# Attention loads turned in place, memory loaded into its final tile, and the attention and routing of a quad gathered ahead of product 1

## The chip, the cores and the metric

The kernel runs on 1 core of a Trainium2 chip. The metric is the device time of one execution in microseconds (us); lower is better. PE is TensorE, PEld its weight loads, DVE is VectorE, ACT is ScalarE, POOL is GpSimd, and SP is the engine whose queue issues every DMA of this kernel.

## The reference, cut to what matters

All data is float32; x is 8 x 1024 x 1024, and each of the 8 batches has its own memory of 64 rows and a mask over them.

```python
scores = einsum('bsd,bmd->bsm', layernorm(x), memory) * scale   # masked, softmax over m
x = x + einsum('bsm,bmd->bsd', softmax(scores), memory)
h = layernorm(x)
base   = einsum('btd,od->bto', h, weight)
probs  = softmax(h @ router_w.T)            # 8 experts, the best 2, renormalised
Ax     = einsum('nd,erd->ner', h, lora_A)   # rank 16 for each expert
out    = x + base + 2 * einsum('ner,ne,eor->no', Ax, w_dense, lora_B)
```

## The kernel before, in words

**Tiles, pairs, quads.** The 8192 rows are 64 tiles of 128 rows. Two tiles are a *pair* (32 of them, four to a batch). After a start (`first`, pairs 0 and 1), the function `quad(u)` (L1128) works on the two pairs u and v = u+1 in one pass; it runs 15 times, for u = 2, 4, ..., 30. The dense product h x weight is done by Strassen's scheme in two levels: per quad seven *joint* products (`joint`, L817), run in the order 1, 2, 6, 3, 7, 5, 4, each of seven blocks of matmuls in two PSUM banks (named jl and ju). The sums that the products need are made by POOL (`rt_sums` L632, `rt_sum_3` L643, `joint_sums_steps` L793), and DVE, ACT and POOL take the results away. Product 1 leaves its result in the tile of its own operand (hA): the first part is copied there by ACT (L839), two others by DVE (L841), and matmuls of the same product reuse the bank only after such a copy.

**What one quad does.** Three generations of pairs are in flight. u and v: the two low-rank and router products (`rt_low_rank_tile`, L576), the choice of the experts (`rt_top`, L588: 15 small DVE operations and one ACT Exp in the middle), the turn of the scaled low-rank rows (`rt_turn_low_rank`, L617), a low-rank add of one quarter of the output (`eight`, L751), and the seven products. n = u+2 and m = u+3: the end of the attention (softmax of m, `att_turn_p`, readout = probabilities x memory, `att_add` into x), then layernorm 2 and the write and blocked re-read through DRAM (`f_rows`, `norm_send`, `norm_fetch`) that lets DVE turn h (`rt_turn_tile`). f = u+4 and g = u+5: the load of x in blocked form (`load_xs`, L96), its turn by DVE (`att_turn_tile`, L393), and the scores (`att_scores`, L400).

**What sets the order.** `tc.manual_schedule` (L1332): each engine, and SP's DMA queue, executes its instructions strictly in the order in which the program writes them. Tiles come from pools with a fixed number of buffers; an instruction that needs a buffer waits until its last reader is done. `ring` (5 buffers of 128 x 1024) holds the blocked loads xs, the turned x (xT), h on its way out, the re-read hs, and the blocked memory ms. `ps_at` and `ps_rt` are one PSUM buffer each: `ps_at` holds in turn the scores of f (sct), their turned form (sc) and turned probabilities; `ps_rt` holds the low-rank result (pa) and m's turned probabilities. Hooks are functions that `joint` calls between its blocks: with them the softmax of m (L1196, L1197) and the last turn of g (L1201) are put between blocks of product 1.

**Order in a late quad before** (u = 4 to 26; u = 2 is "early", u = 28 and 30 are the tail). PE: the last product's end of the quad before (`pending`), low-rank of u, the turn of m's scores (sc), low-rank of v, product 1, `rt_turn_low_rank(u)`, `eight(u)`, readout of n, turned probabilities of m, scores of f and g, readout of m, `rt_turn_low_rank(v)`, `eight(v)`, product 2, and so on. DVE: `rt_top(u)`, turns of f0 and f1, the shift of m's scores (L434, L439), turn of g0, product 1's copies mixed with the division of m's softmax and the turn of g1, then the adds. SP: at product 4 the first half of the output rows of u and v (two stores), `fetch_sums("w11")` (L696), the two x tiles of g, the blocked tiles f0, f1 and g0; then the second half of the output rows (two stores, `last`, L1323), then g1 and the two x tiles of f.

**Memory.** For a new batch `load_ms` (L343) loads the memory in blocked form into a ring slot, with runs of 1 KB, `turn_mem` (L353) turns it into memT, and `centre_turned` (L361) takes off the row means.

Of the kernel before, what the change touches and what calls it, by code (L numbers as in the profile page):

```python
# [17 lines left out]
P = 128  # L18
# [6 lines left out]
def kernel(  # L25
# [35 lines left out]

    const = ctx.enter_context(tc.tile_pool(name="const", bufs=1))
    xpool = ctx.enter_context(tc.tile_pool(name="xpool", bufs=10))
    ring = ctx.enter_context(tc.tile_pool(name="ring", bufs=5))
    turned = ctx.enter_context(tc.tile_pool(name="turned", bufs=2))
    sums = ctx.enter_context(tc.tile_pool(name="sums", bufs=1))
    memp = ctx.enter_context(tc.tile_pool(name="memp", bufs=2))
# [11 lines left out]
    def load_blocked(dst, rows):  # L79

        v = rows.rearrange("(t i) d -> i t d", i=NB)
        for q in range(4):
            nc.sync.dma_start(  # L83
                out=dst[q * NB : (q + 1) * NB], in_=v[:, :, q * QD : (q + 1) * QD]
            )
# [219 lines left out]

    mcs, mem_ts = {}, {}

    def mem_stats(b: int):
        mv = small.tile([P, 2], F32, tag="mv_mem", name=f"mv_mem_{b}", bufs=2)
        row_stats(mv[:M], mems[b][:M], f"mem_{b}", M)  # L310
        mcs[b, "mv"] = mv

    def centre_mem(b: int, chunks: bool):

        m = mems[b]
        if (b, "mv") not in mcs:
            mem_stats(b)  # L320
        mc = ring.tile([P, D], F32, tag="ring", name=f"memc_{b}_{chunks}")
# [13 lines left out]
    def turn_mem_pe(b: int, chunks: bool, mc):  # L335
# [4 lines left out]
        mem_ts[b, chunks] = mt  # L340
        return lambda: nc.scalar.copy(mt, tr)

    def load_ms(b: int):  # L343

        msr = ring.tile([P, D], F32, tag="ring", name=f"ms_{b}")
        n = M // NB * QD
        ms = msr[:, :n].rearrange("p (t c) -> p t c", c=QD)
        load_blocked(ms, mem[b])
        ones = msr[:, n : n + P]
        nc.gpsimd.memset(ones, 1.0 / D)  # L350
        mcs[b] = ms, ones, msr[:, n + P : n + P + M]

    def turn_mem(b: int):  # L353

        mt = memp.tile([P, KD, M], F32, tag="memT", name=f"memT_{b}_True", bufs=1)
        ms, ones, of_k = mcs[b]
        transpose_blocked(mt, ms)
        nc.vector.tensor_reduce(of_k, mt.rearrange("p k m -> p m k"), AX.X, ALU.add)
        mem_ts[b, True] = mt

    def centre_turned(b: int):  # L361

        _, ones, of_k = mcs.pop(b)
# [19 lines left out]

    def xT_tile(u: int, r: int):
        t = ring.tile([P, KD, P], F32, tag="ring", name=f"xT_{u}_{r}")
        x_ts.setdefault(u, []).append(t)
        return t

    def att_turn_pe(u: int, r: int, later: bool = False):
# [1 line left out]
        return transpose_pe((t[:, :KH, :], t[:, KH:, :]), xts[u][r], f"x{u}_{r}", later)  # L391

    def att_turn_tile(u: int, r: int):  # L393
        transpose_blocked(xT_tile(u, r), xss[u][r])

    def att_turn(u: int):
        for r in range(2):
            att_turn_tile(u, r)

    def att_scores(u: int, apart: bool = False):  # L400

        mt = mem_ts[u // PPB, u > 1]
        if apart:
            sct = bank_of(f"sct_{u}")[:, :P]
        else:
            sct = ps_at.tile([2 * M, P], F32, tag="at", name=f"sct_{u}")
        for k in range(KD):  # L410
            for r in range(2):
                mm(  # L412
                    sct[r * M : (r + 1) * M, :], mt[:, k, :], x_ts[u][r][:, k, :],
                    start=(k == 0), stop=(k == KD - 1),
                )
# [37 lines left out]
    def att_divide(u: int):  # L453
        s, of_s = ps[u]
        den, rden = of_s[:, 1], of_s[:, 2]
        nc.vector.reciprocal(rden, den)
        tt(s, s, rden.unsqueeze(2).to_broadcast([P, 2, M]), ALU.mult)
        ps[u] = s

    def att_turn_p(u: int, in_place: bool = False):  # L460
        if in_place:
            ptp = ps_rt.tile([2 * M, P], F32, tag="rt", name=f"ptp_{u}")
        else:
            ptp = ps_at.tile([2 * M, P], F32, tag="at", name=f"ptp_{u}")
# [81 lines left out]
    def hb_tile(u: int, r: int):  # L546
        if r == 0:
            h_tiles(u)
        t = turned.tile([P, KH, P], F32, tag="hB", name=f"hB_{u}_{r}", bufs=5)
        hbs[u].append(t)  # L550
        return t

# [17 lines left out]
            rt_low_rank_tile(u, r)  # L570

    def rt_low_rank_copy(u: int):
        axls[u] = small.tile([P, 2, ER + E], F32, tag="axl", name=f"axl_{u}", bufs=1)
# [84 lines left out]


    quarters, kept = {}, {}  # L660
    shared = const.tile([P, 3, HK, HH], F32, name="shared")

    def quarter(w, i: int, j: int):
        return w[:, i * HK : (i + 1) * HK, j * HH : (j + 1) * HH]
# [463 lines left out]
    def quad(u: int):  # L1128
# [25 lines left out]
            rt_low_rank_tile(u, 0)  # L1154
        rt_low_rank_tile(u, 1)
        if early:
            att_divide(n)
            att_turn_p(n)
            for r in range(2):
                rt_turn_tile(v, r)  # L1160
            rt_sums(v)
        rt_top(u)
# [6 lines left out]
        if early:  # L1169
            att_turn(m)  # L1170
        js_one, js_two = joint_sums_steps(1, u)
        js_one()
        rt_sum_3(u)
        rt_low_rank_tile(v, 0)
        if late and far:
            att_turn_tile(f, 0)
            load_xs(g, (1,))
            att_turn_tile(f, 1)
        if early:
            load_xs(f)  # L1180
        elif far:
            load_xt(f)
        rt_low_rank_tile(v, 1, later=True)
        rt_sum_3(v)
        js_two()
        if late:
            att_rstd(m)
            att_shift(m)
            if far:
                att_turn_tile(g, 0)  # L1190
        if early:
            att_scores(m)

        hooks = {2: [], 5: []}
        if late:
            hooks[2].append(lambda: att_exp(m))  # L1196
            hooks[5].append(lambda: att_divide(m))  # L1197
        if early:
            hooks[2].append(lambda: att_sc(m))
        elif far:  # L1200
            hooks[5].append(lambda: att_turn_tile(g, 1))  # L1201
        end_1 = joint(1, u, hooks, aside=not more)
        end_1()
        joint_sums(2, u)
        t_add(0, 0, u, v)
        still_one()
        rt_turn_low_rank(u, bank_of(f"trw_{u}")[:, : 2 * P])
        rt_low_rank_copy(v)
        eight(u)
        if early:  # L1210
            load_xs(g, (0,))
            att_rstd(m)
            att_exp(m)
            att_divide(m)
            att_turn_tile(f, 0)
            load_xs(g, (1,))
            load_xt(f)
            att_turn_tile(f, 1)
            att_turn(g)
        if more:  # L1220
            att_readout(n)
            att_turn_p(m, True)
        eight_add(u)
        if more:
            att_add(n)
        rt_top(v)
        if far:
            att_scores(f)
            att_scores(g, True)
        if next_mem:  # L1230
            load_ms((f + 2) // PPB)
        if more:
            att_readout(m)
            f_sums(n)
        if new_mem:
            load_mem(b)
        if more:
            att_add(m)
        rt_turn_low_rank(v, bank_of(f"trw_{v}")[:, : 2 * P])
        eight(v)  # L1240
        eight_add(v)

        hooks = {2: [], 5: []}
        if more:
# [135 lines left out]
```

## Time and profile before

| what | us |
| --- | --- |
| median of 3 runs (lowest to highest) | 1235.64 (1234.27 to 1235.87) |
| the profiled execution's own time | 1235.62 |
| span of that execution | 1233.8 |
| PE busy in the span | 1133.7 |
| DVE busy | 831.1 |
| POOL busy | 654.2 |
| ACT busy | 557.3 |
| mean granted TensorE clock | 0.968 |

The profiled execution agrees with the median, so what is read in it can be set against the runs. A quad takes some 75 us: the first low-rank matmul of the quad u = 16 starts at 640.15 us of the span, that of u = 18 at 714.87. Times within a quad are given below from that first low-rank matmul. Shares over the span average stages that differ, so a change in one stage is read from the timeline of that stage: what each engine does there, and which wait ends last.

### The profile page before, as it was taken

How to read it: one execution, taken by the hardware profiler on the slowest of the kernel's cores; microseconds unless marked ns; L12 is line 12 of the kernel's file. 1: busy time of each engine (PE TensorE's matmuls, PEld its weight loads, DVE VectorE, ACT ScalarE, POOL GpSimd, SP SyncE). 2: the span in 40 equal slices, each digit the busy share in tenths (PEclk: the TensorE clock that was granted, in tenths of full speed). 3: DMA queues.
4: the chain of work that ended last, by engine and by line, in shares of the span. 5: the costliest groups of instructions: out<-in, count | busy, mean ns of one | idle time of the engine just before them, and what ended most of it. 6: DMA issues, size and time to landing. Idle time of an engine off the chain costs nothing.

```text
span 1233.8 us, 17966 instructions
## 1 busy us (share of the span) xinstructions
PE 1133.7 (92%) x6044; PEld 892.2 (72%) x6044; DVE 831.1 (67%) x1979; ACT 557.3 (45%) x1063; POOL 654.2 (53%) x723
## 2 busy tenths in 40 slices
PE   8997898998989899898998989989898998989988
PEld 6555686885867768686786868868687786876867
DVE  7765668577684866858677585866858567565745
ACT  4584443725437353563625437253473625535000
POOL 0188385463654736556463664636547264564645
PEclk9999998998999989999999999999899998999989
DMA  9777347372565716547364482726637264432401
GB/s 235 176 214 226 99 145 222 126 237 82 178 189 162 230 69 213 159 158 237 93 208 137 149 252 100 226 85 205 197 123 242 81 207 151 137 136 85 164 26 69
DMA packets 109387, 198.42 MB, mean 161 GB/s; under 512 B 13424, under 2 KB 77936, under 8 KB 109296
## 3 DMA queue, kind: packets, MB, share of 16 engines
q1 hardware_dynamic: 109296, 197.28, 51.6%
q8 instruction: 48, 0.79, 0.3%
q14 instruction: 43, 0.35, 0.1%
HBM read 130.65 MB, written 66.58 MB: 160 GB/s over the span
## 4 chain that ended last, share of the span: by engine, by line
PE 70%; DMA 11%; DVE 8%; ACT 5%; issue 3%; SPq 2%; POOL 2%; DVEq 0%; ACTq 0%; POOLq 0%
PE jl L717 26%; PE ju L717 20%; DMA xs<-in_x_dram 6%; PE sct L412 5%; PE eight L709 3%; PE ju L709 3%; PE ro L480 3%; PE jl L709 3%; ACT junk L243 3%; PE pa L582 2%; PE plain L717 2%; DMA out_dram<-xt 2%; SPq L83 2%; DMA xt<-in_x_dram 2%; DVE xt L847 2%
## 5 line engine op out<-in xcount | busy, mean ns | idle before, releaser
L766 POOL TENSOR_TENSOR xt<-xt,hA 128x512 f32<-128x512 f32 x120 | 149.8, 1274 | 150.5 <-DVE hA L843 90.9
L847 DVE TENSOR_TENSOR xt<-jl,xt 128x256 f32<-128x256 f32 (+1 forms) x301 | 139.7, 484 | 131.4 <-PE jl L717 109.2
L717 PE MATMUL ju<-w,s_j 128*128 128x256 f32 x480 | 132.0, 399 | 32.0 <-DVE hA L841 31.8
L804 POOL TENSOR_TENSOR s_j<-s 128x256 f32<-128x256 f32 x45 | 32.8, 728 | 234.4 <-PE jl L717 204.3
L195 ACT ACTIVATE junk<-xt 128x1024 uint8<-128x1024 f32 x60 | 63.0, 1049 | 152.9 <-DMA xt<-in_x_dram 152.2
L717 PEld LDWEIGHTS ju<-w,s_j 128*128 128x128 f32 x480 | 89.8, 196 | 54.0 <-DVE hA L841 36.6
L847 DVE TENSOR_TENSOR xt<-ju,xt 128x256 f32<-128x256 f32 (+1 forms) x150 | 79.6, 547 | 43.2 <-PE ju L717 36.2
L843 DVE TENSOR_TENSOR hA<-jl,hA 128x256 f32<-128x256 f32 (+1 forms) x135 | 68.8, 510 | 55.6 <-PE jl L717 55.2
L638 POOL TENSOR_TENSOR s<-hA,hB 128x512 f32<-128x512 f32 x31 | 39.5, 1274 | 122.2 <-DVE hB L89 65.5
L296 ACT ACTIVATE h<-xt,of_f 128x1024 f32<-128x1024 f32 x60 | 71.3, 1235 | 58.9 <-DVE of_f L292 45.0
L706 DVE TENSOR_TENSOR xt<-ro,xt 128x512 f32<-128x512 f32 x128 | 82.1, 684 | 18.7 <-PE ro L480 18.7
L717 PE MATMUL ju<-t,s_j 128*128 128x256 f32 x360 | 93.8, 383 | 0.0
L582 PE MATMUL pa<-art_sb,hA 128*128 128x136 f32 x512 | 72.3, 285 | 8.2 <-ACT axl L574 7.9
L582 PEld LDWEIGHTS pa<-art_sb,hA 128*128 128x128 f32 x512 | 65.8, 192 | 13.3 <-ACT axl L574 11.2
L717 PEld LDWEIGHTS ju<-t,s_j 128*128 128x128 f32 x360 | 64.1, 190 | 15.4 <-issue 5.2
L89 DVE STREAM_TRANSPOSE xT<-xs 128x1024 f32<-128x1024 f32 x60 | 73.9, 1235 | 0.6
L582 PE MATMUL pa<-art_sb,hB 128*128 128x136 f32 x512 | 70.7, 281 | 0.0
L843 DVE TENSOR_TENSOR hA<-ju,hA 128x512 f32<-128x512 f32 (+1 forms) x75 | 43.4, 578 | 39.4 <-PE ju L717 39.4
L204 ACT ACTIVATE junk<-xt,of_x 128x1024 uint8<-128x1024 f32 x60 | 68.9, 1148 | 1.9
L253 ACT ACTIVATE junk<-xt,of_f 128x1024 uint8<-128x1024 f32 x60 | 68.9, 1149 | 1.5
L412 PE MATMUL sct<-xT,memT_True 128*64 128x128 f32 x960 | 60.6, 284 | 7.6 <-DVE xT L89 7.6
L582 PEld LDWEIGHTS pa<-art_sb,hB 128*128 128x128 f32 x512 | 65.0, 192 | 0.0
(215 smaller groups left out, 2668.7 us busy)
## 6 DMA issues: line engine op xcount, KB each, us to landing
xt<-in_x_dram SPq DMA_DIRECT2D x64, 512.0 KB, 5.6
out_dram<-xt SPq DMA_DIRECT2D x62, 512.0 KB, 3.2
xs<-in_x_dram SPq DMA_DIRECT2D x240, 128.0 KB, 4.5
hd<-h SPq DMA_DIRECT2D x60, 512.0 KB, 2.7
hs<-hd SPq DMA_DIRECT2D x240, 128.0 KB, 3.2
shared<-q_t SPq DMA_DIRECT2D x15, 768.0 KB, 5.1
shared<-q_w SPq DMA_DIRECT2D x14, 768.0 KB, 5.8
mem<-in_ctx_dram SPq DMA_DIRECT2D x16, 256.0 KB, 3.9
```

Source lines behind the costliest of these rows:

```text
L89: nc.vector.transpose(dst.rearrange("p k (t i) -> p t k i", i=NB), src.rearrange("p t (k i) -> p t k i", i=NB),)
L204: nc.scalar.activation(nowhere, xts[u][r], AF.Square, bias=nm[:, r, :], accum_out=ss[:, r, :],)
L253: nc.scalar.activation(nowhere, xts[u][r], AF.Square, bias=nm[:, r, :], accum_out=ss[:, r, :])
L296: nc.scalar.activation(h, xts[u][r], AF.Identity, bias=nmr[:, r, :], scale=rstd[:, r, :])
L412: mm(sct[r * M : (r + 1) * M, :], mt[:, k, :], x_ts[u][r][:, k, :], start=(k == 0), stop=(k == KD - 1),)
L582: mm(pa[:, r, :], h, art_sb[:, k, :], start=(k == 0), stop=(k == KD - 1))
L706: tt(xc, bank, xc, ALU.add)
L709: mm(bank, axwts[u][:, r, :], lb_sb[:, c0 : c0 + n], start=alone, stop=True, skip_group_check=True)
L717: mm(bank, a[:, k, :], w[:, k, :], start=(start and k == 0), stop=(k == n - 1), skip_group_check=True)
L766: nc.gpsimd.tensor_tensor(xc, xc, t_of(p), ALU.add)
L843: tt(t, src, t, ALU.add)
L847: tt(xc, src, xc, ALU.add)
```

## The change

1. `att_turn_tile` turns the blocked x tile in its own ring slot; the scores matmul reads it through a view with 32-element runs, so no second slot (xT) is taken. 
2. `load_ms` loads the memory straight into memT by 8 DMAs with runs of 32 elements (128 bytes) in place of 4 with 1 KB; `turn_mem` turns it in place. The column of ones has a tile of its own, and the start's centred memory uses the tile `shared`.
3. `ring` has 4 buffers in place of 5, hB 6 in place of 5, axl 2 in place of 1.
4. In `quad`, all four turns of f and g stand ahead of POOL's sums for product 1; readout of n, softmax of m, scores of f and g, `rt_top` of u and of v, turned probabilities and readout of m all stand ahead of product 1, which has no hooks any more; both `rt_turn_low_rank` and both `eight` follow it.

```diff
-    ring = ctx.enter_context(tc.tile_pool(name="ring", bufs=5))
+    ring = ctx.enter_context(tc.tile_pool(name="ring", bufs=4))
...
     def load_ms(b: int):
-        msr = ring.tile([P, D], F32, tag="ring", name=f"ms_{b}")
...
-        load_blocked(ms, mem[b])
...
+        mt = memp.tile([P, KD, M], F32, tag="memT", name=f"memT_{b}_True", bufs=1)
+        for q in range(4):
+            for t in range(M // NB):
+                nc.sync.dma_start(
+                    out=mt[q * NB : (q + 1) * NB, :, t * NB : (t + 1) * NB],
...
     def att_turn_tile(u: int, r: int):
-        transpose_blocked(xT_tile(u, r), xss[u][r])
+        t = xss[u][r]
+        v = t.rearrange("p t (k i) -> p t k i", i=NB)
+        nc.vector.transpose(v, v)
+        x_ts.setdefault(u, []).append(t.rearrange("p t (k i) -> p k t i", i=NB))
...
-                    sct[r * M : (r + 1) * M, :], mt[:, k, :], x_ts[u][r][:, k, :],
-                    start=(k == 0), stop=(k == KD - 1),
+                    sct[r * M : (r + 1) * M, :].rearrange("m (t i) -> m t i", i=NB),
+                    mt[:, k, :], x_ts[u][r][:, k], start=(k == 0), stop=(k == KD - 1),
```

The late quad (u = 4 to 26) after the change, by the program:

```python
        rt_low_rank_tile(u, 0); rt_low_rank_tile(u, 1)
        x_sums(m, (1,)); x_squares(m); x_root(m); att_sc(m)
        load_xs(g, (1,)); load_xt(f)
        att_turn(f); att_turn(g)              # was split around and inside product 1
        rt_sum_3(u); js_one()
        rt_low_rank_tile(v, 0); rt_low_rank_tile(v, 1)
        rt_sum_3(v); js_two()
        att_readout(n)                        # was after product 1
        att_rstd(m); att_exp(m); att_add(n); att_divide(m)
        att_scores(f); att_scores(g, True)    # were after product 1
        rt_top(u); rt_top(v)                  # u: was ahead of product 1; v: after it
        load_ms(...)                          # for a new batch
        att_turn_p(m, True); att_readout(m); f_sums(n); load_mem(b); att_add(m)
        end_1 = joint(1, u, {}); end_1(); joint_sums(2, u); t_add(0, 0, u, v)
        rt_turn_low_rank(u); rt_turn_low_rank(v)
        eight(u); eight_add(u); eight(v); eight_add(v)
        end_2 = joint(2, u, hooks)            # from here as before
```

More of the change, by code (lines that the diff above doesn't have):

```diff
@@ L306 @@
     mcs, mem_ts = {}, {}
+    shared = const.tile([P, 3, HK, HH], F32, name="shared")
     def mem_stats(b: int):
@@ L320, in centre_mem @@
             mem_stats(b)
-        mc = ring.tile([P, D], F32, tag="ring", name=f"memc_{b}_{chunks}")
+        mc = shared.rearrange("p q k o -> p (q k o)")[:, :D]
         nc.vector.tensor_scalar(
@@ L341, in turn_mem_pe @@
         return lambda: nc.scalar.copy(mt, tr)
+    ones = const.tile([P, P], F32, name="ones")
+    nc.gpsimd.memset(ones, 1.0 / D)
     def load_ms(b: int):
-        msr = ring.tile([P, D], F32, tag="ring", name=f"ms_{b}")
-        n = M // NB * QD
-        ms = msr[:, :n].rearrange("p (t c) -> p t c", c=QD)
-        load_blocked(ms, mem[b])
-        ones = msr[:, n : n + P]
-        nc.gpsimd.memset(ones, 1.0 / D)
-        mcs[b] = ms, ones, msr[:, n + P : n + P + M]
-    def turn_mem(b: int):
[L355 to L359, printed above, removed]
+        mt = memp.tile([P, KD, M], F32, tag="memT", name=f"memT_{b}_True", bufs=1)
[3 more added lines that the diff above has]
+                    out=mt[q * NB : (q + 1) * NB, :, t * NB : (t + 1) * NB],
+                    in_=mem[b, t * NB : (t + 1) * NB, q * QD : (q + 1) * QD].rearrange(
+                        "i (k c) -> i k c", c=NB
+                    ),
+                )
+        mem_ts[b, True] = mt
+    def turn_mem(b: int):
+        mt = mem_ts[b, True]
+        turn = mt.rearrange("p k (t i) -> p (k t) i", i=NB)
+        nc.vector.transpose(turn, turn)
+        mcs[b] = small.tile([P, M], F32, tag="of_k", name=f"of_k_{b}")
+        nc.vector.tensor_reduce(mcs[b], mt.rearrange("p k m -> p m k"), AX.X, ALU.add)
     def centre_turned(b: int):
-        _, ones, of_k = mcs.pop(b)
+        of_k = mcs.pop(b)
         mt = mem_ts[b, True]
@@ L385, in xT_tile @@
         t = ring.tile([P, KD, P], F32, tag="ring", name=f"xT_{u}_{r}")
-        x_ts.setdefault(u, []).append(t)
+        x_ts.setdefault(u, []).append(t.rearrange("p k (t i) -> p k t i", i=NB))
         return t
@@ L548, in hb_tile @@
             h_tiles(u)
-        t = turned.tile([P, KH, P], F32, tag="hB", name=f"hB_{u}_{r}", bufs=5)
+        t = turned.tile([P, KH, P], F32, tag="hB", name=f"hB_{u}_{r}", bufs=6)
         hbs[u].append(t)
@@ L572, in rt_low_rank_copy @@
     def rt_low_rank_copy(u: int):
-        axls[u] = small.tile([P, 2, ER + E], F32, tag="axl", name=f"axl_{u}", bufs=1)
+        axls[u] = small.tile([P, 2, ER + E], F32, tag="axl", name=f"axl_{u}", bufs=2)
         nc.scalar.copy(axls[u], pas.pop(u))
@@ L660 @@
     quarters, kept = {}, {}
-    shared = const.tile([P, 3, HK, HH], F32, name="shared")
     def quarter(w, i: int, j: int):
@@ L1156, in quad @@
         if early:
-            att_divide(n)
-            att_turn_p(n)
             for r in range(2):
@@ L1161, in quad @@
             rt_sums(v)
-        rt_top(u)
+            att_divide(n)
+            att_turn_p(n)
+            att_turn(m)
         if late:
@@ L1168, in quad @@
             att_sc(m)
-        if early:
-            att_turn(m)
+            if far:
+                load_xs(g, (1,))
+                load_xt(f)
+                att_turn(f)
+                att_turn(g)
+        rt_sum_3(u)
         js_one, js_two = joint_sums_steps(1, u)
         js_one()
-        rt_sum_3(u)
         rt_low_rank_tile(v, 0)
[L1175 to L1178, printed above, removed]
+        rt_low_rank_tile(v, 1)
+        rt_sum_3(v)
+        js_two()
         if early:
             load_xs(f)
-        elif far:
-            load_xt(f)
[L1183 to L1211, printed above, removed]
+            att_scores(m)
+        if more:
+            att_readout(n)
+        if early:
+            load_xs(g)
+            load_xt(f)
+            att_turn(f)
+            att_turn(g)
+            att_sc(m)
+        if more:
             att_rstd(m)
             att_exp(m)
+            att_add(n)
             att_divide(m)
[L1215 to L1226, printed above, removed]
         if far:
@@ L1229, in quad @@
             att_scores(g, True)
+        rt_top(u)
+        rt_top(v)
         if next_mem:
@@ L1232, in quad @@
         if more:
+            att_turn_p(m, True)
             att_readout(m)
@@ L1238, in quad @@
             att_add(m)
-        rt_turn_low_rank(v, bank_of(f"trw_{v}")[:, : 2 * P])
-        eight(v)
-        eight_add(v)
+        end_1 = joint(1, u, {}, aside=not more)
+        end_1()
+        joint_sums(2, u)
+        t_add(0, 0, u, v)
+        still_one()
+        for p in (u, v):
+            rt_turn_low_rank(p, bank_of(f"trw_{p}")[:, : 2 * P])
+        for p in (u, v):
+            eight(p)
+            eight_add(p)
         hooks = {2: [], 5: []}
```

## The prediction

> **What bounds the kernel now.** I read the page's shares first, then its chain, the waits of PE, and the timelines of one quad (u = 16). The chain that ended last, shares of the span by engine:
>
> ```profile
> PE 70%; DMA 11%; DVE 8%; ACT 5%; issue 3%; SPq 2%; POOL 2%; DVEq 0%; ACTq 0%; POOLq 0%
> ```
>
> PE carries it, but not alone: 11% are loads. PE's waits (total us, times, longest):
>
> ```profile
> PE ju L717 <- DVE hA L841: 31.8, 12, 2.7
> PE eight L709 <- ACT axwt L626: 18.5, 30, 0.8
> PE jl L717 <- ACT hA L839: 10.6, 13, 0.8
> ```
>
> The first and third are product 1 waiting for its copies. PE's timeline shows the place (start, duration, wait before it):
>
> ```profile
> 650.90 1.03 PE L717 MATMUL ju<-w,s_j 128*128 128x256 f32 x4
> 652.75 1.13 PE L717 MATMUL jl<-shared,s_j 128*128 128x256 f32 x4 [0.82 <-ACT hA L839]
> 656.53 1.80 PE L717 MATMUL ju<-w,s_j 128*128 128x256 f32 x4 [2.65 <-DVE hA L841]
> 658.12 1.91 PE L717 MATMUL jl<-shared,hA 128*128 128x256 f32 x4
> ```
>
> A block of four takes 0.86 where nothing is waited for. Product 1 takes 648.31 to 659.83, 11.5 us for 7 x 0.863 = 6.0: **5.5 us lost**, partly by waits, partly because two blocks run at half speed. DVE was the late one: choosing experts for u beside POOL's sums (7.1 us, 644.54 to 651.63, against 2.6 for v), then turns. Now the other side, SP:
>
> ```profile
> 647.40 0.86 SPq L907 DMA_DIRECT2D out_dram<-xt  x2
> 648.31 3.02 SPq L83 DMA_DIRECT2D xs<-in_x_dram  x4
> ```
>
> and, for those four loads (the last of the blocked tiles, g1), from the tile view:
>
> ```profile
> DMA to landing us min/median/max: 3.7/4.2/4.7
> ```
>
> The last of the four is issued at 650.8 and lands at 654.8. DMA is busy 0.93 of 632.9 to 657.4: the burst of stores and loads is bound by its bytes, not by who issues it. DVE turns g1 only at 657.12, and PE asks for it at
>
> ```profile
> 664.13 3.71 PE L412 MATMUL sct<-xT,memT_True 128*64 128x128 f32 x64
> ```
>
> So the load has 6 us to spare today. That slack is what the change spends.
>
> **The change, step by step, in a late quad.** Let t = 0 be the quad's first low-rank matmul (640.15). Low rank of v ends at t = 8.16; product 2 starts at 671.89, t = 31.74 (mean of the twelve quads u = 4 to 26: 31.80). PE's work between is product 1 6.0, two turns of low-rank rows 0.5, two eights 1.7, two readouts 3.8, scores 3.7: 15.8 of 23.6, so 7.8 are lost there and the change could gain most of them.
>
> *What it removes.* Product 1's 5.5 us (DVE and POOL will be done with sums and turns before it), and one of two waits at eight (0.8, with 0.2 beside it).
>
> *What it puts in their place.* DVE meets all four turns ahead of everything else. The burst is issued in the same order (two stores still precede g1), so g1 lands at t = 14.67 (the same reading in the twelve quads: 14.3 to 15.9, mean **14.88**). Behind g1's turn DVE holds, in its order: the shift of m's scores, n's adds, the division, both choices of experts, m's adds. PE holds readout of n (done at t = 10.1), then f's scores. These need the PSUM buffer that m's turned scores hold until the shift has read them, so even f, loaded long before, waits for g1: idle from 10.1 to about 16.8. Then turned probabilities and readout of m, then product 1. ACT holds the copy of those probabilities behind both Exps of the choices, so readout of m waits for the choice for v to begin. From g1's landing:
> - turn 1.24 (row of 657.12) and 0.05: 1.3
> - reciprocal, two shifts, maximum (653.99 to 655.02): 1.0
> - n's four adds (one row of four, at 140.21): 2.5; the Exp of m (0.8) lies beside them
> - division (656.73 to 657.20): 0.5
> - choice for u, POOL now quiet (665.77 to 668.39): 2.6
> - choice for v up to its difference (0.4), Exp (0.2), copy of the probabilities (0.3) and its weights: 1.0
> - readout of m 1.9; product 1 without a stall 6.0
> - first turn to first eight 0.84 (1108.15 to 1108.99), two eights 1.7: 2.6
>
> That is 18.9 and some half dozen handovers of 0.05 to 0.1, say **19.4**. Product 2 starts at 14.88 + 19.4 = 34.3 against 31.8: **+2.5 us in each of 12 quads, +30**.
>
> *Clock.* In 656.5 to 660, after the 2.65 us wait, the granted clock was 0.55:
>
> ```profile
> 656.50:660.00 3.50, 3.47 (x9) 2.71 (x10) 1.82 (x4) 0.00 (x0) 0.47 (x1) 0.55 0.03 12
> ```
>
> The new 6.7 us wait will bring this too. It falls on the scores: 3.7 us from t = 16.8 end at 20.5, while the copy they precede is ready at 23.2 by DVE's chain, so 2.7 us of slowing are hidden. The half-speed stretches in this trace that follow a wait last 3.4 to 6.8 us, costing 1.7 to 3.4: I take 0.2 a quad (+2), with 1.7 as the other end.
>
> [...]
>
> *Turning in place, strided scores.* DVE's turn writes and reads the same 1024 elements: 1.24 as now. The matmul with 32-element runs is in no row. Nearest: the scores' own 57 ns per matmul, so 0 at one end (and no gain: same columns); doubled, +3.7 a quad at the other, of which 2.7 are hidden: +1.0. I take 0, since DVE's turns, which today write in such runs, show 1.24 for 1024 elements and 0.67 to 0.70 for 512, no surcharge.
>
> *Memory in 128-byte runs.* Six quads load it after the scores, some 10 us before the turn in product 2: hidden. At the start `turn_mem` follows closely (issue 82.7, turn 86.7, PE needs the means at 88.95). Eight issues instead of four cost 1.8 us on SP; packets, 4 times as many, between a quarter and all of the time of a 1 KB packet each. PE then waits 1 to 4 us: **+2**.
>
> [...]
>
> *Ring of 4, hB 6, axl 2.* After in-place turns the quad needs four slots: h leaves its slot before hs comes. hs of m takes slots just sent, so SP waits no more than now. axl 2 frees little: the low-rank PSUM buffer is still single, so PE's 0.37 us there stays.
>
> *Ends.* u = 2 has no burst and gains product 1's place in order; its loads of g wait for m's scores, the same chain follows, product 2 about 143 to 146 against 147.3: -3. u = 28 has no loads, but the chain readout, shift, adds, two choices stands ahead of product 1: t = 31.7 against 29.3: +2.4. u = 30 loses a 4.1 us wait for the choice for v, and the half speed after it: -6.
>
> Sum: 30 + 2 + 2 - 3 + 2.4 - 6 = +27.4. The profiled time is 1235.62, the median 1235.64: **1263**.
>
> **Rivals.**
> 1. *The clock or the strided scores land on the path* (1.0 to 1.7 more in each of 12 quads: +12 to +20): **1275 to 1283**. For it: any half speed left at readout of m and product 1 is paid in full; against: 2.7 us of cover.
> 2. *Faster: the last tile is not what DVE waits for.* If the burst, freed of waits on ring slots, brings g1 when g0 comes today (mean t = 10.0), each quad starts product 2 at 29.4, -2.4: 12 x -2.4 - 5 = **1201**. It decides at a landing of t = 12.4, 2.5 us earlier than read. Against: DMA is already 0.93 busy, and two stores stay ahead of g1.
> 3. *A wash*: landing about 2 us earlier, or the choices shorter: **1236**.
> 4. *The ring of 4 does not do what it says*: f's loads now wait for n's turned slots; if they move the burst by 1 us, +12: **1275**.
>
> **How the numbers follow.** Forecast (1250 to 1274) 0.62; rival 1 0.16; rival 4 0.09; wash 0.05; faster 0.08. Faster by over 0.2% (about what a measurement can tell from no change): 0.09; within 0.2%: 0.02; slower: 0.89. The low end allows a per-quad cost of 1.2 (1247), the high end rivals 1 and 4 with the upper prices: 1246 to 1286.
>
> **What would show it.** Right: in the profile after, product 1 has no wait for L841's copies; PE has one wait of 5 to 7 us ahead of f's scores, released by DVE's shift or turn, and one of up to 3 ahead of readout of m, released by ACT; loads of xs have a larger share of the chain; quads of some 77.5 us. Wrong: g1 lands well before t = 12.4; scores longer than 3.7 us at full clock; product 1 still waits for DVE (m's adds stand just ahead of its copies); a clock below 0.96.

## The result, and the profile after

| what | before | after |
| --- | --- | --- |
| median of the runs (lowest to highest), us | 1235.19 (1234.27 to 1235.87), 4 runs | 1294.11 (1286.94 to 1301.11), 4 runs |
| the profiled execution's own time | 1235.62 | 1301.11 |
| span of that execution | 1233.8 | 1299.2 |
| mean granted TensorE clock | 0.968 | 0.945 |

The ratio after to before is 1.048 (95% interval 1.042 to 1.054): slower, as forecast, but by 59 us where 27 were forecast, and beyond the range's end of 1286. The readings below are of the profiled execution, the longest of the four. All lines of the code below are those of the changed kernel or of the experiment.

The chain of work that ended last, after, shares of the span by engine:

```profile
PE 83%; issue 7%; DVE 4%; ACT 2%; DMA 2%; POOL 1%; SPq 0%; DVEq 0%; ACTq 0%
```

DMA has fallen from 11% to 2% of the chain and PE has grown by 13 points; "issue", time for which the profile shows no wait, is 7%. The prediction had named a larger share of loads as a sign of being right; that sign failed, though this view can't carry it: it puts the new wait ahead of the scores down to "issue" (81.4 us, 6.3% of the span) and does not follow it back to a load. Where PE stands idle is told by its waits (total us, times, longest):

```profile
PE sct L424 <- issue: 81.4, 12, 8.1
PE ro L492 <- ACT s L483: 36.2, 14, 2.9
...
PE eight L720 <- ACT axwt L638: 3.7, 15, 0.3
```

The waits of before are gone: product 1 has none for its copies (31.8 and 10.6 us before), eight's fell from 18.5 to 3.7. In their place stand 6.8 us ahead of the scores in each of twelve quads, and up to 2.9 ahead of readout of m. What releases the scores is seen on DVE, in the quad u = 16 (starts at 674.41):

```profile
689.33 1.25 DVE L405 STREAM_TRANSPOSE xs<-xs 128x1024 f32<-128x1024 f32 x1 [3.45 <-DMA xs<-in_x_dram]
...
690.73 0.48 DVE L446 SCALAR_TENSOR_TENSOR s<-sc,of_x,bias 128x64 f32<-128x64 f32 x2
```

DVE turns g1 as soon as it has landed, then shifts m's scores until 691.21, and PE's scores start at 691.31. DVE's waits, the two that matter:

```profile
DVE xs L405 <- DMA xs<-in_x_dram: 100.0, 48, 5.5
...
DVE of_top L619 <- ACT of_top L610: 30.8, 14, 3.0
```

The first is DVE waiting for loads, expected. The second is new, 2.2 us on average in 14 quads (1.4 to 3.0 in the twelve late ones), and not in the prediction: the choice of the experts stands still in its middle, waiting for ACT's Exp. The timeline of ACT in the quad u = 16 says why:

```profile
694.85 0.27 ACT L429 COPY scts<-sct 128x128 f32<-128x128 f32 x1 [2.51 <-PE sct L424]
696.59 0.27 ACT L429 COPY scts<-sct 128x128 f32<-128x128 f32 x1 [1.48 <-PE sct L424]
696.76 0.21 ACT L610 ACTIVATE of_top<-of_top 128x2 f32<-128x2 f32 x1
698.94 0.20 ACT L610 ACTIVATE of_top<-of_top 128x2 f32<-128x2 f32 x1 [1.98 <-DVE of_top L609]
699.05 0.25 ACT L483 COPY s<-ptp 128x128 f32<-128x128 f32 x1
```

ACT's order is: copy of f's scores, copy of g's scores, Exp of the choice for u, Exp of the choice for v, copy of m's probabilities. DVE in the same quad:

```profile
694.50 0.16 DVE L609 TENSOR_TENSOR of_top<-top 128x2 f32<-128x2 f32 x1
...
697.00 0.17 DVE L619 TENSOR_SCALAR of_top<-of_top 128x2 f32<-128x2 f32 x1 [1.55 <-ACT of_top L610]
```

The operand of the first Exp was ready at 694.66, but the Exp ran at 696.76, behind both copies, that is behind PE's last score. And the scores were slow. PE in the same quad:

```profile
691.31 5.25 PE L424 MATMUL sct<-xs,memT_True 128*64 128x128 f32 x64 [6.66 <-issue]
696.49 0.33 PE L478 MATMUL ptp<-ident,s 128*128 128x128 f32 x1
699.35 1.99 PE L492 MATMUL ro<-mem,s 64*128 64x512 f32 x8 [2.54 <-ACT s L483]
701.27 1.13 PE L728 MATMUL jl<-shared,hA 128*128 128x256 f32 x4
```

The scores take 5.25 us where they took 3.71 before; product 1 then runs without a stall in this quad. The windows of the idle stretch and of the scores (length, busy us of PE, PEld, DVE, ACT and POOL, granted clock, DMA share, GB/s):

```profile
684.60:691.30 6.70, 0.05 (x2) 0.02 (x1) 3.07 (x6) 1.38 (x2) 1.81 (x2) 0.71 0.87 287
691.30:696.60 5.30, 5.29 (x65) 5.13 (x65) 4.01 (x17) 1.04 (x6) 0.00 (x0) 0.72 0.02 3
```

The granted clock over the scores is 0.72, and loads cannot be the reason: DMA is at 0.02 there. Last, two groups of the page:

```profile
L424 PE MATMUL sct<-xs,memT_True 128*64 128x128 f32 x960 | 84.2, 350 | 90.2 <-issue 81.4
...
L405 DVE STREAM_TRANSPOSE xs<-xs 128x1024 f32<-128x1024 f32 x60 | 74.1, 1241 | 100.2 <-DMA xs<-in_x_dram 100.0
```

(busy us, mean ns of one, idle us just before them). One matmul instruction of the scores takes 350 ns (284 before); whether by the clock or by the strided operand, this line can't tell. The turn in place takes 1241 ns (1235 into another slot before): no surcharge.

Where the 65.5 us between the two profiled executions lie: twelve late quads of 80.54 instead of 74.90 us, +67.7; u = 2 +0.9; u = 28 +3.0; u = 30 -5.8; the start -0.4; sum +65.4. From product 2 to its end a late quad takes what it took before, 43 us. So the question is one of some 37 us at the head of a quad.

### The profile page after: what moved, and what is told of

Its sections match the earlier page's. It is cut to its first block, busy times and chain, and to the rows that moved or that the text cites. A ratio compares the mean times of both kernels' runs of the same rounds, so it can differ in the third digit from the quotient of the medians.

```text
span 1299.2 us, 18123 instructions
## 1 busy us (share of the span) xinstructions
PE 1137.3 (88%) x6044; PEld 910.7 (70%) x6044; DVE 773.7 (60%) x1979; ACT 556.7 (43%) x1063; POOL 651.6 (50%) x717
## 4 chain that ended last, share of the span: by engine, by line
PE 83%; issue 7%; DVE 4%; ACT 2%; DMA 2%; POOL 1%; SPq 0%; DVEq 0%; ACTq 0%
PE jl L728 28%; PE ju L728 20%; PE pa L594 9%; PE sct L424 7%; PE ro L492 5%; PE jl L720 3%; PE ju L720 3%; PE eight L720 2%; PE plain L728 2%; DMA xs<-in_x_dram 1%; PE j L728 1%; PE ch L728 1%; DVE xt L858 1%; DVE axl L627 1%; SPq L83 0%
## 5 line engine op out<-in xcount | busy, mean ns | idle before, releaser
L815 POOL TENSOR_TENSOR s_j<-hB 128x256 f32<-128x256 f32 x30 | 21.8, 725 | 295.6 <-PE jl L728 295.6
L424 PE MATMUL sct<-xs,memT_True 128*64 128x128 f32 x960 | 84.2, 350 | 90.2 <-issue 81.4
L424 PEld LDWEIGHTS sct<-xs,memT_True 128*64 128x64 f32 x960 | 80.5, 187 | 102.4 <-issue 102.2
L405 DVE STREAM_TRANSPOSE xs<-xs 128x1024 f32<-128x1024 f32 x60 | 74.1, 1241 | 100.2 <-DMA xs<-in_x_dram 100.0
L728 PE MATMUL ju<-w,s_j 128*128 128x256 f32 x480 | 124.2, 381 | 0.3 <-DVE xt L858 0.3
L296 ACT ACTIVATE h<-xt,of_f 128x1024 f32<-128x1024 f32 x60 | 71.3, 1235 | 66.8 <-DVE of_f L292 58.9
L728 PEld LDWEIGHTS ju<-w,s_j 128*128 128x128 f32 x480 | 86.7, 189 | 18.0 <-DVE xt L858 1.5
```

The lines of the kernel that those rows point to most:

```text
L296: nc.scalar.activation(h, xts[u][r], AF.Identity, bias=nmr[:, r, :], scale=rstd[:, r, :])
L405: nc.vector.transpose(v, v)
L424: mm(sct[r * M : (r + 1) * M, :].rearrange("m (t i) -> m t i", i=NB), mt[:, k, :], x_ts[u][r][:, k], start=(k == 0), stop=(k == KD - 1),)
L728: mm(bank, a[:, k, :], w[:, k, :], start=(start and k == 0), stop=(k == n - 1), skip_group_check=True)
```

## The experiments

**Theory A**, formed from the lines above: the wait for g1 throttles PE, the scores run slowly, the Exps of the choices stand behind their copies on ACT, so DVE's chain from g1's landing to readout of m grows by some 2 us, and in some quads readout of m and product 1 still run at half speed. **Rival B**: scores that read runs of 32 elements are slow by themselves. **Rival C**: the ring of 4 makes loads wait. The table holds the means over the quads u = 4 to 26, counted from the quad's first low-rank matmul, and the time in the whole span from 100 us on at half clock. Each ratio is to runs of the kernel before that were measured beside that kernel (medians of 1233.3 to 1234.8 us for the experiments), and differences to the kernel before in the text are to these:

| kernel | median, us | ratio to before (95%) | g1 lands | readout m | product 2 | quad | half clock |
| --- | --- | --- | --- | --- | --- | --- | --- |
| before (as above) | 1235.19 | | 14.88 | 27.67 | 31.80 | 74.90 | 80.7 |
| after | 1294.11 | 1.048 (1.042 to 1.054) | 14.91 | 25.74 | 37.47 | 80.54 | 146.3 |
| e1_warm | 1338.13 | 1.083 (1.080 to 1.086) | 15.22 | 29.86 | 40.59 | 83.66 | 23.1 |
| e2_exp_first | 1266.10 | 1.024 (1.022 to 1.026) | 15.24 | 24.10 | 34.83 | 77.91 | 115.0 |
| e3_g1_early | 1273.87 | 1.031 (1.029 to 1.033) | 12.68 | 23.54 | 35.04 | 78.11 | 112.6 |
| e4_old_order | 1231.66 | 0.997 (0.996 to 0.998) | 15.43 | 27.65 | 31.78 | 74.85 | 81.5 |
| e5_warm_short | 1262.86 | 1.024 (1.022 to 1.027) | 14.59 | 23.44 | 34.17 | 77.24 | 23.4 |
| e6_exp_warm | 1270.79 | 1.033 (1.027 to 1.039) | 14.79 | 23.32 | 34.73 | 77.80 | 44.9 |
| e7_exp_g1 | 1232.22 | 1.000 (0.998 to 1.002) | 12.15 | 20.85 | 31.58 | 74.65 | 81.3 |
| e8_product_first | 1262.83 | 1.024 (1.022 to 1.026) | 12.27 | 19.84 | 33.05 | 76.35 | 101.7 |
| e9_shift_first | 1224.64 | 0.991 (0.989 to 0.993) | 12.57 | 20.13 | 31.34 | 74.41 | 64.6 |
| e10_product_first2 | 1217.40 | 0.986 (0.982 to 0.990) | 12.26 | 19.84 | 27.04 | 72.99 | 61.0 |
| e11_eight_early | 1186.97 | 0.963 (0.961 to 0.965) | 11.81 | 19.83 | 26.99 | 70.98 | 24.1 |

### e1_warm: PE kept busy through the wait

```diff
+        if late and far:
+            keep_warm(55, ident)
         if far:
             att_scores(f)
             att_scores(g, True)
...
+            if late and far:
+                keep_warm(12, ident)
             att_turn_p(m, True)
```

> The changed kernel with 55 spare matmuls (128 columns each) on PE ahead of f's scores and 12 ahead of the turned probabilities of m, in the late quads, so that PE does not stand idle while it waits for g1; nothing else is touched. Theory A (half clock: the 6.9 us wait throttles PE, the scores then run at half speed, the Exps of the choices stand behind their copies on ACT, and in some quads the half speed reaches readout m and product 1): the 64 matmuls of the scores go back from 5.2 to about 3.7 us, readout of m starts some 8.8 to 9.3 us after g1's landing instead of 10.0 to 11.4, product 1 holds its 6 us everywhere; 1250 to 1268 us. Rival B (scores with runs of 32 elements are slow by themselves, 350 ns against 284 ns a matmul at any clock): the scores keep some 5 us, 1285 us or more.

1338 us: far above theory A's range, and inside rival B's ("1285 us or more"), but for another reason. PE's timeline shows a wrong dose: each spare matmul is two instructions of 0.114 us, so the 55 took 12.55 us, nearly twice the wait of 6.8. (The expectation for e5 calls 0.114 us the time of a spare matmul; it is that of one of its two instructions.)

```profile
706.19 12.55 PE L178 MATMUL idle<-ident 128*128 128x128 f32 x110
718.66 3.71 PE L424 MATMUL sct<-xs,memT_True 128*64 128x128 f32 x64
```

The second line decides something all the same: with PE kept busy (mean granted clock 0.992 in this run, 0.945 in the changed kernel) the strided scores take 3.71 us for 64, the time before the change to the hundredth. **Rival B falls**; the 350 ns went with the granted clock, 0.72 over the scores of the changed kernel's quad u = 16.

### e2_exp_first: the Exps ahead of the copies of the scores

```diff
         if far:
-            att_scores(f)
-            att_scores(g, True)
+            copies = att_scores(f, False, True), att_scores(g, True, True)
         rt_top(u)
         rt_top(v)
...
             att_turn_p(m, True)
+            if far:
+                for do in copies:
+                    do()
             att_readout(m)
```

> The changed kernel with the two copies of the scores of f and g put behind the copy of m's probabilities on ACT, so that the Exps of both choices no longer stand behind the scores. Theory A: DVE's wait for the Exp of the choice for u (30.8 us in the span) goes, readout of m starts 1.0 to 1.5 us earlier a quad, the half clock itself stays: 1272 to 1284 us. If ACT's order is of no weight and only PE's half speed counts: 1288 to 1296 us.

1266 us, 28 us less than the changed kernel, more than theory A gave it. In the quad that starts at 657.47, PE and then ACT:

```profile
674.75 5.91 PE L424 MATMUL sct<-xs,memT_True 128*64 128x128 f32 x64 [7.04 <-issue]
680.59 0.33 PE L480 MATMUL ptp<-ident,s 128*128 128x128 f32 x1
681.37 1.99 PE L494 MATMUL ro<-mem,s 64*128 64x512 f32 x8 [0.45 <-ACT s L485]
```

```profile
678.14 0.20 ACT L612 ACTIVATE of_top<-of_top 128x2 f32<-128x2 f32 x1 [2.36 <-DVE of_top L611]
680.75 0.20 ACT L612 ACTIVATE of_top<-of_top 128x2 f32<-128x2 f32 x1 [2.40 <-DVE of_top L611]
681.05 0.27 ACT L485 COPY s<-ptp 128x128 f32<-128x128 f32 x1
```

The scores are as slow as ever (5.91 us), but nothing waits for them: the first Exp runs while PE is still at it, the second 0.1 us after the last score, both as soon as DVE has made the operand, and PE waits 0.45 us ahead of readout of m instead of 2.5. Product 1 follows 1.92 us after the start of that readout in every late quad. DVE's wait for the Exp of u went from 30.8 us to 2.4, that of the quad u = 30; in the twelve late quads none is left.

### e3_g1_early: g1's load ahead of the second-half stores

```diff
-                load_xs(g, (1,))
                 load_xt(f)
...
-                load_xs(g + 2, (0,))
+                load_xs(g + 2)
```

> The changed kernel with the load of g1 issued beside that of g0 at the end of the quad before, ahead of the four stores of the second halves. Theory A (the chain runs from g1's landing): g1 lands 2.5 to 3.5 us earlier (t near 12), product 2 starts earlier by as much or more, as PE's idle wait gets shorter: 1245 to 1262 us. Rival (the chain is DVE's choices and sums, whatever the load does, or the later stores hold up f's and the next quad's tiles): product 2 stays at t = 37, 1285 us or more.

1274 us, 20 below the changed kernel, less than the number given; but the step is what theory A wants: g1 lands 2.23 us earlier, product 2 starts 2.43 earlier. The rest of the forecast gain was a hope that a shorter wait would take the half clock away; 113 us of it are left. DVE's wait for the loads:

```profile
DVE xs L405 <- DMA xs<-in_x_dram: 73.8, 49, 6.5
```

### e4_old_order: the data of the change, the order of before

The body of `quad` up to product 2 is that of the kernel before; all else is as changed.

> The changed kernel's data (x turned in its slot, memory loaded in its final tile, ring of 4, other buffers as changed) with the order of the quad as it was before the change. Theory A (only the order costs): 1230 to 1242 us. Rival B (strided scores cost by themselves, 1 us or more a quad) or rival C (the ring of 4 makes loads wait): 1250 us or more, with scores of over 3.9 us, or loads of g1 landing later than t = 15.

1232 us, 3 us under before: PE's first wait is again the old one,

```profile
PE ju L728 <- DVE hA L852: 31.0, 12, 3.3
```

and the late quads take 74.85 us. Turning in place, strided scores, memory in 128-byte runs and the ring of 4 cost nothing together. g1 lands at t = 15.43 here, half a us later than before and past the 15 that the expectation gave as rival C's sign; in this order the load has time to spare, and in the changed kernel g1 landed at 14.91, as before the change. So **rival C falls** too: the whole loss is in the order. (What the 3 us come from the traces don't show; the two spans are equal.)

### e5_warm_short: the right dose

e1_warm with 26 and 5 in place of 55 and 12.

> As e1_warm, with 26 and 5 spare matmuls instead of 55 and 12: a spare matmul took 0.114 us there, not the 0.055 that its number went by, so that 12.5 us of spare work stood where 6.9 us were idle. Theory A (half clock, and the Exps behind the slowed scores): 64 matmuls of the scores take 3.7 us from t = 17, readout of m starts 8.8 to 9.5 us after g1's landing, product 2 at t = 33 to 35: 1248 to 1268 us. If the clock were of no weight and ACT's order alone made the difference: 1285 us or more.

1263 us, as theory A had it. In the quad that starts at 657.18:

```profile
667.35 6.07 PE L178 MATMUL idle<-ident 128*128 128x128 f32 x52
673.99 3.91 PE L424 MATMUL sct<-xs,memT_True 128*64 128x128 f32 x64 [0.56 <-PE idle L178]
...
680.69 1.99 PE L492 MATMUL ro<-mem,s 64*128 64x512 f32 x8 [1.37 <-ACT s L483]
```

With the scores at full speed (granted clock 1.00 from 671 to 681), their copies hardly hold the Exps up though they still stand ahead of them: DVE waits 0.2 to 0.3 us for the Exp of u in each late quad, where it waited 1.4 to 3.0. So either remedy, the clock or the order on ACT, is enough by itself, and both give nearly the same time (1263 and 1266 us): it took the two together to make the loss.

### e6_exp_warm: both remedies

e2_exp_first with `keep_warm(26, ident)` ahead of f's scores.

> e2_exp_first with 26 spare matmuls ahead of f's scores. Theory A, as e2_exp_first left it (with the Exps ahead of the copies, the slowed scores end before DVE's choices are through, so that the half clock is covered): the same as e2_exp_first within 6 us, 1258 to 1270 us. If the scores' half speed is still paid there: 1240 to 1255 us.

1271 us, theory A's number or a little over, and no gain on e2: the half speed over the scores was covered there. It isn't free, though. With faster scores PE waits behind them instead, and in five quads what comes next runs slowly after that wait of 2.1 to 2.4 us, here readout of m (3.68 instead of 1.99 us):

```profile
366.16 0.33 PE L480 MATMUL ptp<-ident,s 128*128 128x128 f32 x1
368.72 3.68 PE L494 MATMUL ro<-mem,s 64*128 64x512 f32 x8 [2.22 <-ACT s L485]
```

### e7_exp_g1: order on ACT and early g1 together

The edits of e2_exp_first and e3_g1_early.

> e2_exp_first and e3_g1_early together: the Exps ahead of the copies, and g1's load ahead of the stores of the second halves. Theory A (the chain from g1's landing through DVE to readout of m; both are terms of one sum): product 2 at t = 32 to 33, 1234 to 1248 us. If the two remove the same time, or PE's slowed scores become the bound: 1258 us or more.

1232 us, just under the range: the two gains add up and more (28 and 20 were 48, the sum measured is 62). Most of the surplus is g1's landing: 2.23 us earlier in e3 than in the changed kernel, but 3.10 earlier in e7 than in e2. From the landing to product 2 nothing new is gained: e3 takes 22.36 us, the changed kernel 22.56; e7 takes 19.43, e2 19.59. Product 2 starts at 31.58, and the kernel stands level with before.

```profile
649.62 6.41 PE L424 MATMUL sct<-xs,memT_True 128*64 128x128 f32 x64 [3.70 <-issue]
...
656.64 1.99 PE L494 MATMUL ro<-mem,s 64*128 64x512 f32 x8 [0.35 <-ACT s L485]
```

PE's wait ahead of the scores is down to 3.70 us, but they still take 6.41 in this quad.

### e8_product_first: product 1 back behind the low rank

In quads from u = 4 on, DVE and PE get this order (e7 otherwise):

```diff
+            hooks = {2: [], 5: []}
+            if late:
+                hooks[2].append(lambda: att_exp(m))
+                hooks[5].append(lambda: att_divide(m))
+            if far:
+                hooks[5].append(lambda: att_turn_tile(g, 0))
+            end_1 = joint(1, u, hooks, aside=not more)
...
+            rt_top(u)
+            if more:
+                att_readout(n)
+                att_add(n)
```

Behind these come f's scores, readout of m, g1's turn, the turned rows of u, the choice for v, g's scores, sums over n's rows, turned rows of v, m's adds and the eights.

> e7_exp_g1 with product 1 put back directly behind the low rank of v in the quads from u = 4 on, and only the turn of f and the shift of m ahead of its copies on DVE; the choice for u behind product 1, then n's adds, the turn of g1, the choice for v, m's adds; PE has readout of n, scores of f, readout of m and scores of g behind product 1. PE then has no work that waits for g1 until scores of g, near t = 20. Theory A (the time is lost to PE waiting for g1 through one chain of DVE): product 1 without a wait from t = 8.2 to 14.2, product 2 at t = 25 to 29, 1175 to 1215 us. If DVE's own work is the bound whatever its order: 1225 us or more.

1263 us: a miss by 48 at least, and inside the rival's range (DVE's own work, 1225 or more); e10 tests that rival. Product 1 does run at t = 8.15 and its wait is 0.8 instead of 3.5 us, but product 2 is not earlier. PE waits anew, behind product 1:

```profile
672.81 1.72 PE L494 MATMUL ro<-mem,s 64*128 64x512 f32 x4 [1.57 <-DVE xt L719]
...
682.05 1.13 PE L722 MATMUL eight<-lb_sb,axwt 128*128 128x512 f32 x2 [1.60 <-ACT axwt L640]
```

Readout of m needs the PSUM banks that n's adds free, and these stood behind the choice for u; the second eight needs a copy that stood behind ACT's sums over n's rows. Half speed followed the first of these waits in eleven of the twelve late quads and the second in three, 102 us in the span.

### e9_shift_first: only g's scores behind g1

```diff
             att_exp(m)
+            if late and far:
+                att_turn_tile(g, 0)
             att_add(n)
+            if late and far:
+                att_turn_tile(g, 1)
             att_divide(m)
```

with `att_turn(g)` taken out ahead (e7 otherwise).

> e7_exp_g1 with DVE's shift of m's scores ahead of both turns of g, n's adds between these two turns, so that f's scores no longer wait for g1 (they need the PSUM buffer which the shift releases), and only g's scores do. Theory A (what stands behind g1's landing makes the chain): f's scores start near t = 11 instead of 14.3, DVE's adds of n lie ahead of g1's turn; product 2 at t = 29 to 30.5 instead of 31.6, 1205 to 1222 us. If the choices on DVE, not what stands ahead of them, hold up readout of m: 1228 to 1236 us.

1225 us, just above the number given, and slightly faster than before. (One of its four executions took 4037.59 us, for a reason that nothing here shows; the median of the other three is 1223.88, and the ratio is theirs.) f's scores start at t = 11.31 instead of 14.26, but readout of m gains only 0.7 us: DVE now works without a gap from the shift to the choice for v (n's adds, both turns of g, both choices), and PE waits for it in the middle of the scores:

```profile
801.57 2.66 PE L424 MATMUL sct<-xs,memT_True 128*64 128x128 f32 x30 [2.74 <-DVE of_s L470]
```

So DVE's amount of work, not only g1, bounds this order.

### e10_product_first2: the order of e8 mended

```diff
+            if far:
+                att_turn_tile(g, 1)
             if more:
                 att_readout(n)
                 att_add(n)
...
-            rt_top(u)
...
             if more:
                 att_readout(m)
...
+            rt_top(u)
+            rt_turn_low_rank(u)
             rt_top(v)
+            rt_turn_low_rank(v)
...
+        hooks = {2: [], 5: [] if early else [eights_now]}
```

> e8_product_first with the order mended where its trace showed PE waiting again behind product 1: m's probabilities are copied ahead of the choice for u on ACT, n's adds and the turn of g1 stand ahead of that choice on DVE (readout of m waited 1.6 us for n's adds), the copy of v's turned rows stands ahead of the sums over n's rows on ACT (eight waited 1.6 us), the two eights go into product 2, m's adds behind both choices. Theory (e8 lost product 1's gain in new waits on DVE and ACT, which order alone makes): product 2 at t = 27 to 30, 1180 to 1212 us. If DVE's work, 20 us of it between t = 6 and product 2, is the bound in any order: product 2 at t = 31 or later, or product 2 itself stalls for DVE, 1225 us or more.

1217 us, 16 below before. Product 2 starts at 27.04 as forecast, not at 31 or later, so DVE's work was not the bound that e8 had run into; the time is a little over the number given, since the eights only moved and half speed follows the last wait:

```profile
652.79 0.44 PE L638 MATMUL trw<-ident,axl 128*128 128x128 f32 x2 [2.17 <-DVE axl L629]
653.07 1.03 PE L730 MATMUL jl<-w,hB 128*128 128x256 f32 x4
...
654.57 1.91 PE L730 MATMUL jl<-w,hB 128*128 128x256 f32 x4
```

The block at 654.57 takes 1.91 us, that at 653.07 took 1.03: the granted clock is 0.5 from 654.15 on, for 3.41 us, 1.36 us after the wait had ended at 652.79.

### e11_eight_early: an eight in PE's last wait

```diff
+            eight(u)
             rt_top(v)
             rt_turn_low_rank(v)
...
             def eights_now():
-                for p in (u, v):
-                    eight(p)
-                    eight_add(p)
+                eight_add(u)
+                eight(v)
+                eight_add(v)
```

> e10_product_first2 with the eight of u put into PE's last wait, the 2.2 us between the turned rows of u and of v (PE waits there for DVE's choice for v), instead of into product 2. Theory A (PE's waits cost twice, once as time and once as half clock behind them): 0.9 us of PE's work leaves product 2, the wait is cut into two of less than 1 us, and the half speed in product 2's first blocks (3.4 us in ten of twelve quads, 1.7 lost) goes: 1.5 to 2.5 us less a quad, 1188 to 1203 us. If the clock does not follow the length of a wait: 0.9 a quad, 1205 to 1210 us.

1187 us, 0.963 of before (0.961 to 0.965): 46 us faster than before, 107 than the change as made. The wait of 2.17 us is now two of under 0.6:

```profile
641.16 1.13 PE L722 MATMUL eight<-lb_sb,axwt 128*128 128x512 f32 x2 [0.46 <-ACT axwt L640]
642.87 0.44 PE L638 MATMUL trw<-ident,axl 128*128 128x128 f32 x2 [0.58 <-DVE axl L629]
643.15 1.03 PE L730 MATMUL jl<-w,hB 128*128 128x256 f32 x4
```

That is 1 us under the range given for theory A. A quad loses 2.0 us: 0.86 of eight's work that filled the wait, and some 1.1 of half speed that no longer follows (in e10 the nine late quads with half speed behind this wait take 73.4 us, the three without it 71.9; in e11 a late quad takes 71.0). The half clock fell from 61 to 24 us, and the mean granted clock is 0.991.

## Why the prediction was wrong in size

Point by point, by its own steps:

1. *Product 1's waits go*: right. PE's waits for its copies are gone from the late quads.
2. *g1 lands at t = 14.88*: right, 14.91. *PE idles from 10.1 to about 16.8*: right, to 17.02; 6.8 us a quad, released by DVE's shift (691.21 in the quad shown).
3. *Landing to product 2 is 19.4*: **this sum failed**. Measured: 37.47 - 14.91 = 22.56. Yet with the Exps off the copies' back it is 19.59 (e2) and 19.43 (e7), with the clock held 19.58 (e5). So the total of 19.4 was right to 0.2 us for the chain that it describes, and a wait was missing from that chain. Part of this closeness is luck: the listed terms add up to 19.4, not to the 18.9 written under them, so that the half dozen handovers (0.3 to 0.6 us) were left out, and other terms must have been that much too long; which, was not measured.
4. *The clock: "the copy they precede is ready at 23.2 by DVE's chain, so 2.7 us of slowing are hidden"*: **the step that failed.** I set the scores' end (20.5 at full speed) against the copy of m's probabilities, the last thing behind them, and skipped the first: in ACT's order the copies of the scores stand ahead of both Exps. The operand of the Exp for u was ready at t = 20.25 (694.66 in the quad shown), so the cover was about -0.2 us, not 2.7 (in e5, with the scores at nearly full speed, DVE waits 0.2 us), and the slowing went into DVE's chain and from there to readout of m: 10.83 us after the landing instead of 8.86 in e2, +1.97 a quad. The remaining difference to e2 is half speed that reached readout of m and product 1 in five of the twelve quads: +0.70 up to product 1 and +0.30 in it. Together 2.97 of the 3.16 that were missing a quad; the 3.16 over twelve quads are 38 us, the whole distance between 1263 and the profiled 1301 (the other misses cancel: u = 2 and u = 28 +4.5, the start -2.4, the 2 us set down for the clock).
5. *Rival 1* (the clock lands on the path, +12 to +20) was the right mechanism, with too small a price and the wrong way: I had half speed at readout of m in mind, 1.0 to 1.7 us, not a detour through ACT to DVE that costs 2 even where PE is back at full speed in time (granted clock 1.00 from 696.6 to 701.2 in the quad shown).
6. *Strided scores and turning in place at 0*: right (e1: 3.71 us; 1241 ns).
7. *Memory in 128-byte runs +2 at the start*: wrong, -0.4. The first of the eight loads was issued at 80.86 where the old one went at 82.72; the old destination was a ring slot that had first to come free. The last landed at 86.20 (86.50 before): the earlier issue made up for four more issues.
8. *Ring of 4, u = 28, u = 30*: right (e4; +3.0 for 2.4; -5.8 for -6). u = 2 gave +0.9 for -3; the same ACT order stands in it, and explains part: 85.1 us in e2 against 86.8 after.
9. *Rival 2, threshold at a landing of 12.4*: borne out once the missing term is gone: in e7 g1 lands at 12.15 and product 2 starts at 31.58, 0.22 before that of the kernel before.

Why single runs of the changed kernel spread from 1287 to 1301 was not tried. Their mean granted clocks (0.945 to 0.954) vary, and five of twelve quads of the profiled one paid for half speed twice, so the number of quads that pay twice may well make the spread; that is argued, not shown.

## What to carry to other kernels

When a wait is moved, list every instruction behind it on each engine that is fed by the waiting one, in that engine's order, and set the slack by the first of them that somebody needs, not by the last. A PE wait can cost twice where the work behind it is not covered (e10: behind a wait of 2.17 us, late quads with half speed took 73.4 us, those without 71.9), so a wait is best filled with work that has to be done anyway (e11: one wait of 2.17 us became two of under 0.6), and spare work of the wrong dose costs more than the wait (e1: 12.55 us of it for a wait of 6.8). Undoing the order while keeping the data (e4) told in one run which half of a mixed change to keep.

## What was not expected of the hardware

In the traces of the kernels before and after, every half-speed stretch inside the span lasted 3.41, 6.83 or 10.24 us (in the changed kernel twelve of 6.83, five of 10.24 and three of 3.41, and one of 2.9 at the span's end; before, nine of 3.41 and seven of 6.83, and one of 2.16 at the end). Within each of the two traces their starts and ends lie whole multiples of 3.413 us apart, to 0.002. In e10 the stretches that start at 507.38, 579.06 and 654.15 are 71.68 and 75.09 us apart, 21 and 22 times 3.413.

In e10 the same wait of 2.17 us, between the same instructions, is followed by half speed in one quad and not in the next. Set against instants 3.413 us apart through those three starts, its twelve late quads fall in two groups. In nine of them 2.01 us or more of PE's idle time lay between two neighbouring instants (part of it outside this wait in four), and half speed began at the second of them, from 0.40 us before the end of the wait to 1.40 after it; in the other three (u = 6, 8, 10) one of the instants cut the wait, no more than 1.75 us of idle time (by the matmul rows) lay between two, and no half speed followed. In e11, where the two waits last 0.46 and 0.58 us, none of the late quads was slowed. Idle time alone does not tell the groups apart everywhere, though: in e8 1.27 us of it (from 671.54) was followed by half speed. What makes the difference was not tried.

The half clock came again in every late quad of the changed kernel, 146.3 us in its span; taking away what followed from it (e5 against after, 23.4 us of half clock left) was worth 31 us of 1294, 2.4%.
